# Four layers on one core: linear attention through sums of x by k, q and k by transposition, late mask rows summed

## The chip, the cores and the metric

The kernel runs on one core of a Trainium2 chip. The metric is the device time of the program in microseconds (us), as a median over runs. The core's engines are named here as in the profile: PE (TensorE, matmul) with its weight loads PEld, DVE (VectorE), ACT (ScalarE), POOL (GpSimd) and SP (SyncE, which issues most DMA transfers).

## The reference, cut to what matters

Four layers work in turn on two batches of 1024 tokens with 128 channels. Each computes `x = x + s * silu(ffn(xn))` where `xn` is x after a layernorm without gain and `s` is an attention of xn. Three parts of it matter here.

```python
# layer 1, attention: 16 heads of 8 channels
qkv = (x @ W_qkv + b_qkv).reshape(B, N, 3, H, hd).transpose(2, 0, 3, 1, 4)
q, k, v = (qkv[0], qkv[1], qkv[2])
...
attn = jax.nn.softmax(sim, axis=-1)        # sim: scaled q.k plus a term by head
weighted = jnp.einsum('bhnm,bhmd->bhnd', attn, v)

# layer 2, attention: linear, 16 heads of 64 channels
qf = elu_feature_map(q)
kf = elu_feature_map(k)
kv = jnp.einsum('nshd,nshm->nhmd', kf, v)
z = 1.0 / (jnp.einsum('nlhd,nhd->nlh', qf, jnp.sum(kf, axis=1)) + EPS)
y = jnp.einsum('nlhd,nhmd,nlh->nlhm', qf, kv, z)
out = jnp.einsum('nlhm,hmd->nld', y, Wo) + bo

# layer 2, ffn: 127 chosen tokens attend to each other under a mask
m_sel = m[bidx[:, :, None], sel_idx[:, :, None], sel_idx[:, None, :]]
```

The mask has 512 rows, while the sequence has 1024 tokens: an index above 511 reads row (and column) 511.

## The kernel before

**Recording and issuing.** The program does not issue instructions as its functions run. `Record` notes each operation as a unit (matmuls of one kind in a row make one unit), and `Record.order` (line 569) reads a packed string, `ORDER`, that lists all units in the order in which they are to be issued, with a flag for each evacuation of PSUM that says whether ACT or DVE does it. A second string, `PLACES`, gives every tile its buffer. `Record.issue` (line 585) then issues everything from one line, so the profile shows nearly every instruction under L605, and groups are told apart by the names of tiles. Each engine works through its own queue strictly in that order, and waits by semaphores where another engine's result is needed. So the two strings alone decide how the stages of the two batches lie beside each other: the second batch follows the first, and each layer's attention and ffn are mixed. The same holds for the SP queue, which issues nearly all DMA transfers, and for the POOL queue, which issues the indirect gathers of layer 1's experts.

**Arithmetic.** All products are in fp32, with moving tiles of up to 512 columns. PSUM has eight banks of 128x512 (`C.bank`); `C.half` and `C.arr` are SBUF tiles of 128x1048 and 128x1024 out of 35 buffers, `C.t512` one of 21 tiles of 128x512. `C.mm` is a product `lhsT.T @ rhs`, `C.transpose` a PE transposition against the identity, `C.evac` a copy by ACT or DVE. `cols(t)` is the slice of block t of 128 columns. `xn` holds tokens in partitions, 128 at a time, and `xnT` channels in partitions.

**Layer 1 attention (`l1_attn`, line 1206).** It computes `qt` and `kt`, q and k with tokens in partitions, for norms and maxima that give a scale and a shift for each head. Then `prepare(g)` (line 1302) makes q and k once more, for a group g of four heads, with channels in partitions: head j of the group lies in partitions 32j to 32j+7, row 32j+8 holds a one (k) or the shift (q), the rest zero. It multiplies `xnT` by weights that were padded on the host in this way, two products of 128x512 for q and two for k. `attend(g, q, k)` works through 16 rounds, each of four score products (`sim`, one for a head, 32 rows each), four exponentials on ACT (`e`) and four products with v (`av`). `prepare` of the next group is recorded ahead of `attend` of the present one.

**Layer 2 attention (`l2_attn`, line 1561).** It takes the 1024 head channels in two halves (`hf`), four tiles of two heads each. For each of eight token tiles it makes k (`pk`) and v (`pv`), adds the bias and the feature map to k on DVE and ACT (`kf`), and copies v with a column of ones to SBUF (`vs`). Then follow the q features (`qf`), and for each of the four tiles a sum over the eight token tiles, `pkv`, of k by v and of k alone. DVE adds v's bias, masks it to the diagonal blocks of two heads and makes the weights for the normalizers (`kvn`). `pz` multiplies those by qf; the result `z` goes through DRAM (`zd`), is spread over partitions (`zc`), inverted and read back broadcast (`zb`, two transfers for each tile). Then `nd` multiplies qf by the masked k-v sums, DVE multiplies the product by zb into qf, and `wo` applies the output weights.

**Layer 2 ffn (`l2_ffn`, line 1657).** `sel` has a column for each chosen token and a tile of 128x128 for each of the eight token tiles. The mask's rows are gathered by products `sel.T @ mask` into `mr` (tiles 0 to 3 against the mask's rows, tiles 4 to 7 each against `ml`, a copy of row 511 in all partitions), then transposed, and the columns gathered the same way into `ms`.

**`program` (line 2257)** calls the stages; `stage(l2_attn, weights("l2"), v[1], b, r)` passes `xnT` alone.

Of the kernel before, what the change touches and what calls it, by code (L numbers as in the profile page):

```python
# [21 lines left out]
ALU = mybir.AluOpType  # L22
# [234 lines left out]
def pack_inputs(inputs):  # L257
# [40 lines left out]
    "c-m!I2UrwW*Pb&oTj*7#h$!}oHTH%Yup_a?7NfC8W7McDyE80cODwU)9yRvF*n96W_7)WziYSUmhix<WKljd(@B5yA7ucPdTTXe;Iq$hZVE)R<"  # L298
    "E*-f1OU@qa(Fp(qP)<WEIq9kv+i#Hy74GfnT@`P`bEsZnxN}8hVWD?nKw+q$W<ikM=y3{K-0GZB?Nr93Rg)G&M0;G|W8|SXdZ_5pb!E?^!*iiV"
    "PVw>THJ?|l_oxAU%J!=8X?s)$SU<%HAf8kpPH)JrC@RICK6bBC#aQXV;SsN+(tge}BwFlNt3khN=G_wS+UYCPeDZvzPdYW}Mp$v=>t<O(#XAmY"  # L300
    "c0WHLv|_1IydhTH9CQ2ytp4!_g9zG7U7js`_hX-S@cTgc|F3ZmX68Z={Z_SsNDd^dA3dt?&yK4OgKOX7t8M0*zK6xv&v){IdKZ^Z+509;RQP^+"
    "r(Q6YHZ(kn+gEmYIDESO$AB)iZ;Tln>s9IneAN3g#XwdM^o`2;ZJ290KP)6<ewlSX%+7|TlOo>Rjg{OxXQ>8@$I=NY*#VUyt1`S*BmPUQe~gN)"
    "5q^gM*$N;ud)!)>x(xga`d#|iE3Gk%+JujWZ3FNjC%PAUj7^8|l6Cj{WdnGY0eApUczA8_-dbhdYVUseu=fkgD$tSazY_MZ7+LA@(f#pbeCm%~"
    "G-GXOAwXUgSajsd_JjbXMD;CMEJLAJtI!W)U?{*`xYbb=piuaI%JM1um97;s!VbMio8NW%zK<0?esN*s7D%6ZBK_N=Oyby>+422{$1j_zDG;a2"
    "`m)NW{W%jyuZDf^W+@JDP{GUo1?)@xA;f#kJfF6c7hfw<>_N6)W_-J*&34FbVK=I8HYdK>`{I|6uDE-AqaAgc-bs>jmVUT<JZ{_40Ns(}w*cB-"
    "s@J>A8931Qy2BtgsrP7A>vEHQc-J_7zxMSUY%;7Fzh*BOdT2NHCOrK1EWqJDf%Ru!$lQ4#!Kd)&b7y|t1;>PApLaX+>&Tx*IX5S*E-aWB`o7hT"
    "U_NJ0|A5$*O}o1O_$GEwlS<zE%L43uTmJp*VSK`1*V(%l4i1FA2LOr>e%X6Wysq{P{m=vZ<Dta+?4mQaBEQ0&<EwnJ0zxx*zVO)e4@>-e>-@_i"
    "*Nmr<EE?kDn70UE`~v@XVbT{X(@GryLcn<I#$o9G$t%BE4>={myk8)_Ho)CI+3OxTylO_h{1+FY=;N?=xcB`oeb++}(S7(|ID4pqpaS0#c%SSR"
    "kBmAfs^kQ}r*;0WyBaD#fp32v{hKnR%0d|9wJ5gXB2h_rFg$<Ls6d-zeLi@K-X8)#`WFbk#Y7ba63~CAP2uq+sv-}<<)N*20wnCkU9#b;%^Pl>"
    "$qUTuaTIzU;Q<;|Sv7gC=|FC<!ErCz!>;@M2nTxAE<BwIr~EHBc*xfSo6p_)J|!LDMvJA5?>B8nrJbKhge8hS@h8LcDjyb}P{*%{oA}EjK~*X~"  # L310
    "io5&Ws*iqkp2FmxzgzjwDja;`{(_A!U<xd&wenEny#0BjV2RH+uy}g?4y)m(+uM2aBY57d|9Jh7_DeH+cbh9I`TNJN8-4%ASE^l~nq2C0xZ{O^"
    "AIQ_DZ)+BowZE(I0ukVoe}NMwa(@iigH}^M)m*#de0t3npj7lPvyEOLLb%>W!aHs3aXjuw_meq+l^zGhb}<DJUMVC7^IVs2nF4+aKuM`r(4am2"
    "e<uY7az{m3gV)cy)<iI8m}+_6v+*uiwE1~WBY(X^Dev^<kAf(Q4*V5F)#U<_=cD=3r%?GF^I!xhx=Pu6h~VOLLsfAb4BFT;=t^)MuM;uDww>ud"
    "U^I^5>A<gHBL;fdp`E9<!v=HCm#?dqdboVWJU_yh5gj2UKvWC-%M311RG(5`#pVH`P!e1MF1?4{Q-xBYY)#Hwa7=_num!&HDG@!0PIZbpQ2{5f"
    "*SQoCbgH0+WL0(;_;(?Wys%P%c;L=X0}%;tEb+E^*nWV54Uy1wb1WQnfUyL8oq|YI)gU^<Q6HVc_y2$@3UIYjrmBb{@Gf#bPC48Q-+hku0KUZ2"
    "qbLA{we!4F^vkP2MJ7hYFOTpyx`XqfM^GRr52K+StPiP^`68rFt@D70EDR|1YIZOvucB$!RaXV!eSr9}-JtnAd8Z51kslTj5mmr#|EYu4<VEra"
    "^yPIf1L?EZ=*SDMc(XcB)NBZU8X<T%9iBu)tsm7gs4hX(gGvtdLt%XEF5b(Q9ig-9uU9zcn4r856N(j2568vyLE*oa754oQ_YzjizB>y4S>~9X"
    "yro%#^<!an%D#I#>1oskGBL4=Fk_)E^vuMYexH8?K|QU;secTL9GiarCS2XU;NIwseSe+ZeU!SIRBeE%sU!$~`>^{+!bQS2c`<KNUf)ZTqQChq"
    "e`@bGUf+FJ{~dVfP90Vh(37s`l{!zp*`%(xy1m1-Cmml{Q@+|VW>X}2&ZpM{pIg-)x4AXqwhdZ8Rm{^7DGO&t-yig|XZ2jasB@7~FQZ->?GE42"
    "Gl~0t`r5KY5AVW1Rmk)eJhT0Nj)8E$LVNH^n3Z9SvU#iIqmM_vm+||Qm^#6R1;eEYdsAz6nzy0b?tLS-B*aYV5TX0Jdz{~n!I;2_APxup&)<D}"  # L320
    "M;*R>=+{u#Z{)JEUu_+5072aK$WUe1;DcQc8c2*@fFnW&xTKDN13ksxdL1YW2T<$@oBa_0p7tR-mEaFS`2yl0<U{DF>!a^qzYEbYI>A=iBd#Y2"
    "e+<*%UA3%$B{RINva+kqW|-s(B1IL>#z>a8f?r;hwtb5`UT798Y#s{>6B?wimvo+m7D0^|<&UZ8Z~^%BR8!}8{03i@_>t1%d6QQHAMaf=d-Wue"
    "C)CU?6N!rlFPm4Xhv*b^>Y9lq1f=Zku36a|J=Ll3^UW4K52aqbo%c|5h-yp6Zl#q!2z=0j9}toVV)bMA+sdNyZrs``nIS^Ym0@a7QD)T3$idaB"
    "!osP`2EZ~zmmP!0zYts%aDuKWi}_Q2yiz23{asg3)j*rqr8dADg*<=0)L;{!G{{aAZ`{wN!>A6)3CZ;FBRL_rqU;{E-gK%3lMTf_Vd-`1zodC6"
    "`hKIkO%BykoF1MZ-z?fz5TF$K75fRUOI=Vkmj_WX-6&oT%zhZ9p!nE5K>?en3cjEC_8BjuPJed2T9H1`^JU1ZdXJ*Sx8XKh<8*^Z9x|j7yAN-N"
    "$V@1?a(=@VPrk(aMf1o4I2B7u(`!fH%f8+*G9LrJ{<9Zh22p$+LCE1gLGVt`|LWP|PR6wT^`kfSZup1)-KveZL8Ew=6x}>>;6na!>FYj=Rwp$5"
    "a^K}YmR79kFa+GMg6!qh)@kiB=f8Aqd%E@;e#>gd;TELLw5J!&Rm>JF(}iE*Yz&(1#ikS(e7Qyy*Y;;A$;w1Her#!LnEI}Q;Pb3z@y`}&+4lin"
    "NMs^LR)^<)zKM&zS*cFVJ|H~%9)h+%g_5)1WHh|mDtX<#=wnqMiZ5??O-dgyEU9u<ojNy01UC%bKe`D_?zXSpSU7RIYt;?aLAcfVTxXwmRkyF+"
    ">+{^V`33$$%!tNK`q#Q~cHEfRgU1$p_S>vVO<ut0jiYOQw|wQ~m^)A~0UnP9*t#;zGB>8qj+SR?22HL7p+|ZJ__n%M+Utw14GVUTd0^W4>g1HC"
    ">xD(rhVdH&&-w6RV{!C9p6cSxwPQ~CRcT;<-u2G2QGbM;9P&@~MkBZE#W3#S^Stiz$ZsLVf8eQV6?XNsH@S7D>yg_17xKifChxr4jDJ!m=tzM-"  # L330
    "6m@x@2L)fF|6WwT0@d(){NC1{zl-7Beiy6XAqADPh&bx+RU_bP+vk4yI`eXS&xkeE3S-X3oK+m2d7iz3UAtWR5i8YhRrYvg`wk^JiND$okI4_X"
    "T>ZuME)DPgUBB+0`r9(+`~}_(9(H^8u&6cPeDuWTZ{M_hcEGPcb`<(;@kQ&Z#}@_uF^VgJ+<@3`M#)nS^aZ^$f9#h7y>lx)sJSJ6{}=G0R|-1p"
    "c;ftDA4b{VM%n#sknc3D78XrB41G)dv6#5Z4#rd{s$km<ZEKYj6hl}*zVBo22)@*Dwb!L~m+N|z6@{-I`gT3^_PRc<U>A%5VI3ht-H_^K+adm-"
    "3L{SNr22=3F7f4ieM@4~jo9K>Vk=A!udUC8hn1^ru2;9z*9hNB)>-1*Sw3X}g?^j*M!X9v`?U8G@N=T3O{w**rK0V1-Jx4ECRQujsE*wltGoO`"
    "5K2FdjmTO7%YOSj2Wr^%M4t)n_1omx08Iw2csui_Av^0n4hbG?9)s%Dy;)HYPwj2Q^|j$(t)b6zbe-0W{;|ikcz_&d^bE;&ZeeV@pW3HCoBHff"
    ")5a%4Y=g?Kwktm39CA1V0)w9Uk;$ubY7|Y}+_|D5uVjlF#TO0m<UQozY|*1QqAS4WkgO+LR?J9Fc4h4zv`v?mZ%><j>&<=f;htqaG20f-H7$En"
    "&333YAGq(UuuqP_t+lzpkKqwlTi%40BLA%VquK>!hV<I$k<aRWC<;Gb=fSA5CuK2N#<q{H)qXe`G8)63svG0?fB#Jdp9uiFjCV6yUQdL}b%U;)"
    "_no}&BeI5;_k#}1ynNr+GwMXG+no#USgw9%yO0&T>(IJ47mjQ>B-BW^DK#qQ_$uPf@gdu*eD(c=wef%W^NX&n8K2U@_}sf>^>9Tu=~saDSQK5&"
    "e~N|UUE2-$UKO|WYy9l!ysYJCR|mazv>dd@c*LXWq*<=0-qA2ObwuR}=HSvP%dL}5^H+`a`f2XRI<Ate6*ro|$`OT&BRq1wr%f1LfuG*YFmdUp"
    "tgV@jl}qLr9@Y1pIkfd{36@rWq2wGaOiB5EL4Wm3Pv326UT+Ftg=e0^_Gn0`&W8teL769BK(C@&Nn7X5{=0ewfYK#H>hj;^jA<`?|I<t_>+8`_"  # L340
    "bYYIEdu*{!58gC4`iJwKm$cd*e>00L=gvU9rSTUt=FidbXZ$7~9ef<=@E6xWE#t{&UQV0f<veqhSV#SQ=1kXs(yNaLoqPJN<4)4)uEK~K?Od@|"
    "sd#^Hzt}c$n-(msF|<@U`C#VwE!OILo1HVY?s+odK-<x^PME%4@9E$nxnqYB2g*Eib&+p`qKc&vS&6^C2n@(3$9nkNn!e2UEbe`jc-mqvcI`52"
    "!dmZPPp<Njoqk`jY;ya0>)JIbu9?yB!R$ZxHF5m%9o&L?jwa7*<nkf!1qjytHFDRjg|@x_92poY-21%U-q)Wx$C;gFA2#uSmKhsI?QHP8(fvOo"
    "VdA=4s<F)_P@Cnwel+KmvdZ6V**5d1pBD70bB`BXhI&|VpAMa~qDGJSd8g)ns`=?%*gI&Leydu?8yN!vPPWhSEAfDUyR|OHo#=8u_|f=h_iE>Y"
    "|IOP|CM+&^XsG@quuAi_6>GgHEpxTnIP6BPlI*Y`LlIHmmsJZX@%f``z~wfNE0>1e79Q6Q4*h@$!c|tOGn~q({*DiM;PT@8-&s1z<6e_CD~4}t"
    "z_&f$cz@N{v!cV}Ni{LEYP-v=FEziG{pGHq$2}USw^WO_8i&}0M=kiX&6TGy``TZHdx>YdUUb}U$~&U@C#u5dRU{4g2hfr)dPK;8$MC2|!^~U#"
    "e!n>5h9KBlMRbO56O=dn*OQ{w&HDP==hFcG{8@LpAmh~0Gx;SBp;{aLCLvTOwA}u&#naZ=8ExNYReKY8B{Wj-749}Hd^*f{rtQ`i^}42(W{r4U"
    "6LzY)#vgSpuLimrZ5=-7_p{x~9yWR6uqM|B*XGt1FgLjq{Rnvbhi*@QoYL?gogzWnj7hsc8qyZ#j$bvY3ydo?Iy~*w@9TNLko15F%R+NA=l`jH"
    "QR-D#)BCSz{#9ku;>@MX3O+9T;l~BUzw@yYZ^e5;MceXOKTe(z=(rYEX=&okm}#@-Dxzc*Nzj;qb?3O0O7`JfEi)ZkCU{xD3H()<_$u(1ve+95"
    "ieIVD<EL@{$$iUiDYjVKXAi3DJ##mO@Ks2Wt^e6Pcr*E^&m+FhD|>E(w;{plK3S756<4^aE3J`ba5j1z@UX+h$R0mB3^NBnE86YMntw&+PJ4!L"  # L350
    "h&$2jZqiBqTGACb#dop?<#em`;Uquo&HWzA4zIqUt2*bkTIv<_zUzZ$ap`&bvXJ<VEmWQU9O#X<ru^fg{=(r}p2Eepj>plL1+~SEFO*YdU!4iN"
    "(CM;Ztos<EgMu=J@XX@dIuKg+`$2HDxHoU7ct?#MJikulp5FQA<M=B%p3xOf^!yZjB>vAnxxuRbg|X}TE97|h__|?RQlIBFTds#Xr>k@nvL9qs"
    "YO3&tyA1-iRc<KgZbx7DP&2A{xEf#cwtLi8Z9aFrsy}LUtL^4`21m7uH^s(<&x?$;pXuvGz7&uq|Gnh&GcxJ>CHp>IF%HV>c`d^$CoJyQ+J@Y0"
    "ovZRk5*%oMUZ>DtEOZ*}AOA|I^S1KKHkV&rN#v1t39i#IVR=tOK7->>|KsfzN8>{Bh)M#SccQ&`S9Z{?&&0n9eLCD~CR}oLI9d0-tNBfPE90d$"
# [851 lines left out]
def l1_attn(C, w, xnT, b, out):  # L1206
# [88 lines left out]
    scales, shifts = own[:, :G], own[:, G:]  # L1295

    nc.vector.tensor_scalar(shifts, shifts, C.c["row8"], None, ALU.mult)
    bs = C.small("bs", G)
    nc.vector.tensor_mul(bs, scales, w["bq"])
    nc.vector.tensor_add(shifts, shifts, bs)  # L1300

# [78 lines left out]
def l1_ffn(C, w, xn, xnT, b, out):  # L1380
# [177 lines left out]
    out["g"] = acc  # L1558


def l2_attn(C, w, xnT, b, res):


    nc = C.nc
# [801 lines left out]
```

## Time and profile before

| What | Value |
|---|---|
| Median of 3 runs | 1870.38 us (1868.97 to 1874.28) |
| Profiled execution, its own time | 1864.44 us |
| Its span in the profile | 1862.7 us |
| Mean granted TensorE clock | 0.961 |
| Attention of layer 1, first to last ACT instruction of both batches | 384 to 858 us |
| Attention of layer 2, first product `pv` to last `nd` | 854 to 1118 us |
| Matmul records, DVE, ACT and POOL instructions | 15148, 2819, 1988, 440 |

The profile is of one execution. Its page gives the busy time of each engine, the chain of work that ended last (followed back from the end: at each step to what released it), and the costliest groups of instructions. Further views of the same trace give the busy time of each engine in chosen stretches, the instructions in order of time, and all instructions that touch a named tile. A line of a group has the line of code, engine and operation, then out<-in by tile names with buffer numbers left out, shapes, count, the total busy time and the mean length of one in ns, and the idle time of the engine just before them with what ended it. In the order of time each line has its start, its length, and in square brackets the idle time before it with its releaser. The page says of itself that matmuls are pipelined and their ends modelled, so that a busy PE is not PE at its peak.

### The profile page before, as it was taken

How to read it: one execution, taken by the hardware profiler on the slowest of the kernel's cores; microseconds unless marked ns; L12 is line 12 of the kernel's file. 1: busy time of each engine (PE TensorE's matmuls, PEld its weight loads, DVE VectorE, ACT ScalarE, POOL GpSimd, SP SyncE). 2: the span in 40 equal slices, each digit the busy share in tenths (PEclk: the TensorE clock that was granted, in tenths of full speed). 3: DMA queues.
4: the chain of work that ended last, by engine and by line, in shares of the span. 5: the costliest groups of instructions: out<-in, count | busy, mean ns of one | idle time of the engine just before them, and what ended most of it. 6: DMA issues, size and time to landing. Idle time of an engine off the chain costs nothing.

```text
span 1862.7 us, 37413 instructions
## 1 busy us (share of the span) xinstructions
PE 1739.7 (93%) x15148; PEld 1009.8 (54%) x15148; DVE 1335.7 (72%) x2819; ACT 1070.6 (57%) x1988; POOL 416.3 (22%) x440
## 2 busy tenths in 40 slices
PE   7985899679999999999999999999999999899987
PEld 3464456454225842276666668754446776543566
DVE  6775988686213643246889898889987978978865
ACT  4211443136996588856546556766657757766543
POOL 0001110222222143211301370124214510630000
PEclk9895899588999999999999999999999999999989
DMA  3010011002313321242231222101011110001021
GB/s 126 13 23 4 1 24 25 4 1 66 100 40 114 113 70 41 61 151 75 61 89 48 65 67 64 36 1 48 12 37 44 58 47 25 1 1 40 10 73 35
DMA packets 68301, 88.99 MB, mean 48 GB/s; under 512 B 29568, under 2 KB 41856, under 8 KB 68000
## 3 DMA queue, kind: packets, MB, share of 16 engines
q1 hardware_dynamic: 59008, 57.26, 10.2%
q0 software_dynamic: 9120, 29.33, 5.2%
q8 instruction: 119, 1.95, 0.4%
q14 instruction: 54, 0.44, 0.1%
HBM read 79.62 MB, written 6.95 MB: 46 GB/s over the span
## 4 chain that ended last, share of the span: by engine, by line
PE 79%; DVE 10%; issue 4%; ACT 3%; DMA 1%; POOL 1%; SPq 1%; DVEq 0%; POOLq 0%; ACTq 0%
PE sim L605 16%; PE num L605 8%; PE ph L605 6%; PE av L605 6%; PE wo L605 5%; PE tr L605 4%; PE down L605 3%; PE qk L605 2%; PE up L605 2%; PE z L605 2%; DVE u L605 2%; PE p L605 2%; PE nd L605 1%; PE q L605 1%; PE pu L605 1%
## 5 line engine op out<-in xcount | busy, mean ns | idle before, releaser
L605 ACT ACTIVATE e<-sim 128x512 f32<-128x512 f32 (+3 forms) x896 | 427.7, 559 | 148.1 <-PE sim L605 69.0
L605 PE MATMUL num<-e,v 128*64 128x192 f32 (+4 forms) x1280 | 183.7, 426 | 2.2 <-ACT e L605 2.2
L605 DVE TENSOR_TENSOR e<-e 128x512 f32<-128x512 f32 (+3 forms) x320 | 171.6, 574 | 16.4 <-PE num L605 9.1
L605 PE MATMUL sim<-q,k 32*128 32x512 f32 x1024 | 150.2, 638 | 0.5 <-DVE asb L605 0.5
L605 PE MATMUL sim<-q,kT 64*128 64x512 f32 (+3 forms) x768 | 147.7, 504 | 1.5 <-ACT e L605 1.5
L605 POOL TENSOR_TENSOR sq<-qk,tab 128x256 f32<-128x256 f32 x128 | 98.6, 797 | 219.9 <-DVE ss L605 98.5
L605 PE MATMUL av<-e,va 128*32 128x512 f32 x1024 | 134.9, 603 | 0.0
L605 PEld LDWEIGHTS num<-e,v 128*64 128x64 f32 x1280 | 83.1, 138 | 89.9 <-issue 68.1
L605 ACT ACT_TABLE_LOAD x93 | 119.3, 1283 | 9.0 <-DVE h L605 5.2
L605 PE MATMUL ph<-h,w_f 128*128 128x512 f32 x256 | 119.3, 622 | 0.0
L605 PEld LDWEIGHTS sim<-q,kT 64*128 64x128 f32 x768 | 71.7, 186 | 76.9 <-ACT e L605 36.9
L605 PEld LDWEIGHTS sim<-q,k 32*128 32x128 f32 x1024 | 43.9, 183 | 99.8 <-ACT e L605 74.2
L605 ACT ACTIVATE e<-e 128x320 f32<-128x320 f32 (+3 forms) x160 | 76.9, 530 | 30.3 <-DVE e L605 29.7
L605 POOL TENSOR_TENSOR u<-u,sq 128x512 f32<-128x512 f32 x64 | 89.1, 1411 | 0.9
L605 PEld LDWEIGHTS ph<-h,w_f 128*128 128x128 f32 x256 | 50.2, 200 | 60.9 <-issue 58.6
L605 DVE TENSOR_TENSOR sim<-sim,const 128x128 f32<-128x128 f32 x256 | 64.5, 291 | 25.3 <-PE sim L605 24.4
L605 DVE SCALAR_TENSOR_TENSOR conv<-vT,w_a,conv 128x1024 f32<-128x1024 f32 x60 | 78.3, 1312 | 0.9
L605 POOL DMA_INDIRECT we<-in_experts,index x46 | 44.4, 966 | 135.9 <-DVE index L605 42.7
L605 POOL DMA_INDIRECT xg<-xd,index x46 | 45.0, 977 | 122.7 <-DVE index L605 62.0
L605 DVE TENSOR_REDUCE ss<-sq 128x8 f32<-128x512 f32 x96 | 63.1, 675 | 10.3 <-ACT sq L605 9.9
L605 PEld LDWEIGHTS av<-e,va 128*32 128x32 f32 x1024 | 21.5, 108 | 85.1 <-issue 75.7
L605 DVE SCALAR_TENSOR_TENSOR e<-sim,const 128x320 f32<-128x320 f32 (+2 forms) x128 | 60.6, 528 | 8.7 <-PE sim L605 5.7
(535 smaller groups left out, 3576.2 us busy)
## 6 DMA issues: line engine op xcount, KB each, us to landing
zb<-zd SPq DMA_DIRECT2D x192, 128.0 KB
tab<-in_rotary SPq DMA_DIRECT2D x8, 512.0 KB
yd<-y SPq DMA_DIRECT2D x10, 256.0 KB
w_f<-in_f SPq DMA_DIRECT2D x4, 512.0 KB
mk<-in_mask SPq DMA_DIRECT2D x4, 512.0 KB
w_l<-in_l SPq DMA_DIRECT2D x4, 512.0 KB
w_f<-in_f SPq DMA_DIRECT2D x4, 448.0 KB
const<-in_const SPq DMA_DIRECT2D x1, 1041.5 KB
```

What stands on the lines that cost most here:

```text
L605: tc.keep_in_program_order(f(*map(real, args), **{k: real(v) for k, v in kw.items()}))
```

## The change

It has three parts, and a new order.

**Layer 2 attention.** v is no longer made. Since v is x times its weights, the sum over tokens of k by v is the sum of x by k, put through the weights of v. `pg` sums `xn` by kf over the eight token tiles (one product of 128x512 each), `pn` sums kf alone by products with 32 columns of ones, four of them in different column groups. Both are copied to SBUF (`gT`, `kn`); `pkv` multiplies them by the weights and (a 32nd of) the bias of v; DVE masks all four tiles in one operation (`kvT`); `po` multiplies by the output weights, and the copy `kvo` holds the weights from qf straight to the output. `pc` and `kc` make the weights of the normalizers from `kn`. qf is now multiplied by zb itself, without `nd`, and `wo` multiplies it by `kvo`. The tile `vs`, its ones, and `kvn` go. `l2_attn` also takes `xn`.

**Layer 1 q and k.** `prepare` copies four heads out of `qt` or `kt` into a zeroed tile `wide` (zero fill on GpSimd; for k also a fill of ones at place 8), eight tiles of 128 columns, transposes these on PE, and copies the result: q with scale and shift on DVE as before, k by an evacuation on ACT or DVE. The host still packs the padded weights.

**Masks of late rows.** DVE sums the last four tiles of `sel` into `late`; the four products with `ml`, and the four with `lt`, become one each.

**Order.** `ORDER` and `PLACES` are other strings, for all layers.

```diff
-    bs = C.small("bs", G)
-    nc.vector.tensor_mul(bs, scales, w["bq"])
-    nc.vector.tensor_add(shifts, shifts, bs)
 
     def prepare(g):
 
         q, k = C.arr("q"), C.arr("k")
-        for dst, wn in ((q, "wq"), (k, "wk")):
+        for dst, src in ((q, qt), (k, kt)):
+            wide = C.arr("wide")
+            nc.gpsimd.memset(wide, 0.0)
+            wv = wide.rearrange("p (t j c) -> p t j c", j=J, c=32)
+            if src is kt:
+                nc.gpsimd.memset(wv[:, :, :, 8:9], 1.0)
+            sv = src.rearrange("p (t h d) -> p t h d", h=H, d=8)
+            C.evac(wv[:, :, :, 0:8], sv[:, :, J * g : J * g + J, :])
             for i in range(2):
                 s = cols(i, 1, BLK)
                 ps = C.bank("qk")
-                C.mm(ps, w[wn][:, cols(g)], xnT[:, s])
-                if wn == "wq":
+                for t in range(4):
+                    C.transpose(ps[:, cols(t)], wide[:, cols(4 * i + t)])
+                if src is qt:
                     nc.vector.tensor_scalar(dst[:, s], ps, scales[:, g : g + 1], shifts[:, g : g + 1], ALU.mult, ALU.add)
                 else:
-                    nc.vector.tensor_scalar_add(dst[:, s], ps, w["bk"][:, g : g + 1])
+                    C.evac(dst[:, s], ps)
...
-            pk, pv = C.bank("pk"), C.bank("pv")
-            C.mm(pk, xt, w["wk"][:, hs])
-            C.mm(pv, xt, w["wv"][:, hs])
+            pk = C.bank("pk")
+            C.mm(pk, xnT[:, cols(t)], w["wk"][:, hs])
             k, e = C.t512("k"), C.t512("e")
             nc.vector.tensor_add(k, pk, bk[:, hs])
-            nc.scalar.copy(vs[t // 2][:, t % 2, :, 0:P], pv.rearrange("p (a n) -> p a n", a=4))
             nc.scalar.activation(e, k, AF.Exp, bias=C.c["minus1"])
-            nc.vector.scalar_tensor_tensor(kf[t // 2][:, t % 2, :], e, 1.0, k, ALU.min, ALU.max)
+            nc.vector.scalar_tensor_tensor(kt(t), e, 1.0, k, ALU.min, ALU.max)
+            C.mm(pg, xn[:, cols(t)], kt(t), start=t == 0, stop=t == TB - 1)
+            if t % 4 == 3:
+                for c in range(4):
+                    C.mm(
+                        pn[cols(c, 1, 32)], C.c["ones"][:, :32], kt(t - 3 + c), start=t == 3, stop=t == TB - 1,
+                        tile_position=(0, 32 * c), skip_group_check=True,
+                    )
...
+        gT, kn = C.t512("gT"), C.t512("kn")
+        C.evac(gT, pg)
+        C.evac(kn, pn)
+        pkv = C.bank("pkv")
         for a in range(4):
-            pkv = C.bank("pkv")
-            for t in range(TB):
-                C.mm(
-                    pkv[:, :129], kf[t // 2][:, t % 2, cols(a)], vs[t // 2][:, t % 2, a, :],
-                    start=t == 0, stop=t == TB - 1,
-                )
...
+            C.mm(pkv[:, cols(a)], w["wv"][:, at(a)], gT[:, cols(a)], stop=False)
+            C.mm(pkv[:, cols(a)], bv[:, at(a)], kn[:, cols(a)], start=False)
+        kvT, kvo = C.t512("kvT"), C.t512("kvo")
+        nc.vector.tensor_tensor(tiles(kvT), tiles(pkv), C.c["bo64"].unsqueeze(1).to_broadcast([P, 4, P]), ALU.mult)
+        po = C.bank("po")
+        for a in range(4):
+            C.mm(po[:, cols(a)], kvT[:, cols(a)], w["wo"][:, at(a)])
+        C.evac(kvo, po)
+
+        pc, kc = C.bank("pc"), C.t512("kc")
+        for a in range(4):
+            C.mm(pc[:, cols(a, 1, 32)], kn[:, cols(a)], C.c["mean"][:, :32])
+        nc.vector.scalar_tensor_tensor(
+            kc[:, :P].rearrange("p (a n) -> p a n", a=4), pc[:, :P].rearrange("p (a n) -> p a n", a=4), 4.0,
+            C.c["turns"].unsqueeze(1).to_broadcast([P, 4, 32]), ALU.mult, ALU.mult,
+        )
...
-                C.mm(pz[cols(a, 1, 32)], kvs[a][:, P:], qf[a][:, s], tile_position=(0, 32 * a), skip_group_check=True)
+                C.mm(
+                    pz[cols(a, 1, 32)], kc[:, cols(a, 1, 32)], qf[a][:, s], tile_position=(0, 32 * a), skip_group_check=True
+                )
...
             for a in range(4):
-                C.twice(zbs[i][a], zd[2 * a : 2 * a + 2])
-        for i in range(NB2):
-            s = cols(i, 1, BLK)
-            for a in range(4):
-                ps = C.bank("nd")
-                C.mm(ps, kvs[a][:, :P], qf[a][:, s])
-                nc.vector.tensor_mul(qf[a][:, s], ps, zbs[i][a])
+                za = zb[a // 2][:, cols(a % 2, 1, BLK)]
+                C.twice(za, zd[2 * a : 2 * a + 2])
+                nc.vector.tensor_mul(qf[a][:, s], qf[a][:, s], za)
...
-                    C.mm(
-                        ps[:, cols(k)], qf[a][:, cols(4 * g + k)], w["wo"][:, cols(4 * hf + a)],
-                        start=a == 0, stop=a == 3,
-                    )
+                    C.mm(ps[:, cols(k)], qf[a][:, cols(4 * g + k)], kvo[:, cols(a)], start=a == 0, stop=a == 3)
...
+    late = C.t512("late")[:, :P]
+    nc.vector.tensor_reduce(late, sel[:, 4 * P :].rearrange("p (t n) -> p n t", t=4), X, ALU.add)
     ps = C.bank("mr")
-    for t in range(TB):
-        C.mm(ps, sel[:, cols(t)], mks[t] if t < 4 else ml, start=t == 0, stop=t == TB - 1)
+    for t in range(5):
+        C.mm(ps, sel[:, cols(t)] if t < 4 else late, mks[t] if t < 4 else ml, start=t == 0, stop=t == 4)
...
-    for t in range(TB):
-        C.mm(ps[:, :P], mt[:, cols(t)] if t < 4 else lt, sel[:, cols(t)], start=t == 0, stop=t == TB - 1)
+    for t in range(5):
+        C.mm(ps[:, :P], mt[:, cols(t)] if t < 4 else lt, sel[:, cols(t)] if t < 4 else late, start=t == 0, stop=t == 4)
```

## The prediction

> **What bounds the kernel now.** I read the page's busy shares and its chain that ended last first, then busy time by stage, then the order of time inside two stages, then the groups of the instructions that the change touches.
>
> ```profile
> PE 1739.7 (93%) x15148; PEld 1009.8 (54%) x15148; DVE 1335.7 (72%) x2819; ACT 1070.6 (57%) x1988; POOL 416.3 (22%) x440
> ...
> PE 79%; DVE 10%; issue 4%; ACT 3%; DMA 1%; POOL 1%; SPq 1%; DVEq 0%; POOLq 0%; ACTq 0%
> ```
>
> TensorE holds 79% of the chain. But PE's 93% counts the latency of pipelined records, so stages must be told apart:
>
> ```profile
> 450.00:575.00 125.00, 125.00 (x960) 36.04 (x956) 28.39 (x133) 114.55 (x224) 37.02 (x38) 1.00 0.26 79
> 575.00:650.00 75.00, 75.00 (x605) 58.30 (x602) 40.38 (x100) 42.20 (x70) 9.61 (x12) 1.00 0.36 113
> 650.00:800.00 150.00, 149.48 (x1114) 50.78 (x1112) 57.07 (x147) 125.48 (x239) 52.61 (x53) 1.00 0.20 57
> ...
> 850.00:1125.00 275.00, 268.17 (x1476) 172.93 (x1476) 237.23 (x493) 148.81 (x255) 83.81 (x92) 1.00 0.23 68
> 900.00:1050.00 150.00, 149.66 (x810) 97.62 (x808) 137.44 (x304) 79.86 (x130) 15.64 (x16) 1.00 0.26 76
> ```
>
> Columns: stretch, its us, then PE, PEld, DVE, ACT, POOL busy. In 450 to 575 and 650 to 800 (attention of layer 1) ACT is busy 92% and 84%. In 850 to 1125 (layer 2 and the start of layer 3) DVE is busy 237 of 275 us, and in its densest part, 900 to 1050, 137.4 of 150 us (92%) beside a PE that never pauses: two engines near their limit at once. The order of time in layer 1:
>
> ```profile
> 562.12 0.31 PEld L605 LDWEIGHTS sim<-q,k 32*128 32x128 f32 x8 [0.84 <-ACT e L605]
> 562.13 1.14 PE L605 MATMUL sim<-q,k 32*128 32x512 f32 x8
> ...
> 563.20 1.06 PE L605 MATMUL av<-e,va 128*32 128x512 f32 x8
> ...
> 564.19 0.31 PEld L605 LDWEIGHTS sim<-q,k 32*128 32x128 f32 x8 [0.84 <-ACT e L605]
> ```
>
> A round of scores and sums returns every 2.06 us (562.12 to 564.19), exactly four exponentials at the 0.52 us that ACT needs for one (23 in 11.95 us), and the score waits for ACT. PE's own work in a round, 8 sim and 8 av records four abreast, is 4 x 0.43 = 1.7 us. So in these rounds ACT sets the pace. The durations for the sums:
>
> ```profile
> 924.70 3.44 PE nd L605 x8
> 928.13 3.57 PE pkv L605 x32
> ...
> 906.28 1.92 PE L605 MATMUL pz<-qf,kvn 128*32 128x512 f32 x16 [0.28 <-DVE kvn L605]
> 910.46 0.60 PE L605 MATMUL tr<-const,sel 128*128 128x128 f32 x4
> ```
>
> A product is two records (32 products nd are x64), a transposition one. Spacing in a stream: 3.44/8 = 0.43 us per record of 512 columns, 3.57/32 = 0.112 of 128; four transpositions last 0.60 with a latency of 0.27 each, so (0.60-0.27)/3 = 0.11.
>
> **What the Trainium skill says.** "Perfetto Trace Analysis", section Identifying the Most-Contended Engine: matmul busy time is a bad measure of the limit because matmuls are pipelined. The trace agrees: an nd record lasts 594 ns and follows the last by 430. "TensorE: Matmul & The Clock Gate", section Part 3: Packing small matmuls: outputs of 32 columns in different column groups run together. Agrees: 16 pz records take 1.92 us, four abreast, where 16 nd would take 6.9. "Perfetto Trace Analysis", section Optimizing Scalar/DVE Operations: a DVE operand costs more overhead in PSUM than in SBUF. The trace differs: qf<-nd,zb out of PSUM takes 677 ns, q<-q,zb out of SBUF 744; I use the trace. The same section says that GpSimd and DVE share a port; one kvn operation took 1.02 us in place of 0.24 while GpSimd worked on the mask at 902 to 905.
>
> **Layer 2 attention, PE.** Per half of the columns (four in all: two batches, two halves) out go pv, 8 products x 2 x 0.43 = 6.9 us; pkv, 32 x 2 x 0.112 = 7.1; nd, 8 x 2 x 0.43 = 6.9; together 20.9. In come pg, 6.9; pn, 8 products four abreast, 4 x 0.43 = 1.7; the new pkv, 8 x 2 x 0.112 = 1.8; po 0.9; pc, 0.9 at most (32 columns; lower bound near 0, I take 0.9); together 12.2. Four times 8.7 = **34.8 us less**.
>
> **Masks of late rows, PE.** Per batch three mr products (6 x 0.43) and three ms products (6 x 0.112) go: 3.25, so **6.5 us less** for two.
>
> **Layer 1 q and k, PE.** 32 products of 512 go, 64 x 0.43 = 27.5; 128 transpositions of 0.11 come, 14.1: **13.4 us less**. Were a transposition bound at its 0.275 us latency it would be 35 and a loss of 8, but the trace streams them at 0.11. All PE: 54.7 us.
>
> **What the other engines gain or lose.** Layer 2, DVE: the 48 kvn operations go, 16 x (0.391+0.341+0.287) = 16.3; the 32 multiplications by zb cost 0.067 more each, +2.1; kvT 4 x 0.69, kc 4 x 0.29, bv 2 x 0.68, the late sum 2 x 0.675 (as ss from 512 elements), +6.8; in the built program five evacuations of layer 2's second part stand on ACT and not on DVE, -3.4. Net **-10.8 us**. ACT: 32 copies of v go (0.584 each, 18.7), 12 evacuations of gT, kn, kvo come (7.1), net -11.6, of no worth: ACT is busy 54% there. Layer 1: DVE loses 16 additions to k (11.9) and gains copies, slightly less in all, no matter at 23 to 38% busy. ACT gets 7 of 16 copies of k (0.59) and 9 of 16 into wide (256 elements, not in the trace in this form: 0.37 as qkT from 256, at most 0.59), about **+7 us** on the engine that sets the pace. GpSimd: 16 zero fills of 128x1024 at 0.95 (as td) and 8 of ones at about 0.12, 16 us, less the 16 fills of v. They stand in a queue with gathers that wait for indices (longest wait in 450 to 575: 10.4 us); behind them wait the copies into wide, then q and k of the next group. A group is 16 rounds, 33 us, and the next is prepared ahead of it: covered, at nothing. Without that cover each of 8 groups could lose up to 10 us.
>
> **What reaches the end, layer 2.** PE there shrinks by 41.3, DVE by 10.8, so DVE sets the stretch: (237.2-10.8)/0.92, at the fill that 900 to 1050 shows, is 246 us in place of 275: **29 us**. Bounds: PE's 41 if DVE packs to 0.97, and 13 at the mean fill of today (226/0.863 = 262).
>
> **Layer 1.** All of 13.4 if products of the experts can move from 575 to 650 and 800 to 850, where PE is bound, into the rounds' freed slots; -7 if only ACT's extra work counts. I take **6**, a little above the middle: in the built program more products of the experts stand among the first batch's rounds.
>
> The added waits: the new pkv waits for gT and kn, po for kvT, wo for kvo; what is behind them on PE's queue is the next stage's work. The built order puts other products between the first two; a bare hand-over costs about 1 us (an evacuation of 0.6 and latency), some 4 to 8 us at worst, within the bounds. Layers 0 and 3 do the same work in a new written-out order: 0, with 10 us either way. No DMA is added or taken away. Sum **35 us**: the profiled execution, 1864.4 (span 1862.7), would be 1829. Its time is 5.9 below the median shown, so from 1870.4 the forecast is **1835**.
>
> **Rivals.** (A) As summed: 1835, own range 1823 to 1847. (B) PE bounds everywhere: 1870.4-54.7 = 1816. For it: 79% of the chain. Against: ACT's 2.06 us rounds, DVE's 92%. (C) DVE and ACT take over: layer 2 gives 13, layer 1 nothing: 1857. For it: the same two facts. (D) Slower: the normalizers' way by DMA. From z's copy (908.7) to the first multiplication by zb (930.8) it took 22 us in the first half-layer; the nd products, 6.9 us each half, no longer stand in that gap, and now wo waits directly for the multiplications. With half of it exposed in all four halves, 4 x 11 = 44 us, the time is 1835+44 = 1879; it is slower from about 10 us exposed each (35+5.6 over 4). Against it: in the built order 22 to 40 us of PE work, by the spacings above, lie between the last pz and the first multiplication of every half. (E) It does nothing: the freed PE time turns wholly into waiting for ACT and DVE: 1870.
>
> **How the numbers follow.** About 0.3%, 5.6 us, is what a measurement can tell from no change. Chances: A 0.60, B 0.18, C 0.15, D 0.04, E 0.03. Faster 0.92, same 0.04, slower 0.04. The range takes all of A, B's time with the 7 us below it that a better order could bring, and C: 1809 to 1858.
>
> **What would show it.** Right: MATMUL records go from 15148 to 15060 (layer 2 -128, masks -24, layer 1 +64), and the stretch from the first pk to the last wo of layer 2 shortens by some 30 us with DVE over 90% busy; the rounds of layer 1 keep 2.06 us and the layer shortens by less than 10. Wrong: DVE under 85% there with PE waiting for zb or kvo (D, C), or a PE still without pause in layer 2 (B). Layers 0 or 3 changing by more than 10 us would make the sum wrong whatever layer 2 does.

## The result, and the profile after

| | Before | After |
|---|---|---|
| Median | 1871.51 us (4 runs, 1868.97 to 1874.28) | 1848.69 us (4 runs, 1847.05 to 1849.79) |
| Profiled execution, its span, mean clock | 1864.44, 1862.7, 0.961 | 1849.79, 1848.0, 0.951 |

The ratio of after to before is 0.9877 (95% interval 0.986 to 0.9894): 22.8 us less by the medians, where 35 were forecast. The page of the profile after, busy time and the chain that ended last:

```profile
PE 1705.1 (92%) x15060; PEld 996.9 (54%) x15060; DVE 1319.8 (71%) x2769; ACT 1075.4 (58%) x1999; POOL 444.4 (24%) x448
...
PE 43%; DVE 10%; ACT 2%; DMA 2%; issue 2%; SPq 1%; POOL 0%; DVEq 0%; ACTq 0%; POOLq 0%
```

The 88 records that should go are gone. The chain's shares add up to only some 60%, so its 43% can't be set against the 79% of before. Busy time by stage, columns as in the prediction:

```profile
450.00:575.00 125.00, 123.55 (x922) 42.90 (x920) 37.98 (x137) 112.51 (x221) 37.96 (x38) 0.99 0.25 67
850.00:1125.00 275.00, 261.98 (x1514) 167.55 (x1513) 242.02 (x463) 163.42 (x274) 87.39 (x79) 0.99 0.26 73
900.00:1050.00 150.00, 143.12 (x723) 83.16 (x723) 140.75 (x279) 88.96 (x142) 27.73 (x25) 1.00 0.21 59
```

In 900 to 1050, layer 2, PE, which had no pause before, now pauses for 7 us (and its busy time still counts latency), while DVE is busy for 140.75 of 150 us, 94%. The new operations and layer 1's rounds after, as groups and in order of time:

```profile
L604 PE MATMUL pg<-kf,xn 128*128 128x512 f32 x64 | 33.5, 615 | 4.9 <-DVE kf L604 4.5 <-issue 0.4
L604 DVE TENSOR_TENSOR qf<-qf,zb 128x512 f32<-128x512 f32 x32 | 23.7, 764 | 0.6 <-DMA zb<-zd 0.6
L604 PE MATMUL qk<-const,wide 128*128 128x128 f32 x128 | 19.7, 289 | 0.0
L604 POOL MEMSET wide<- 128x1024 f32 x16 | 15.1, 953 | 43.5 <-PE pu L604 23.9 <-DVE g L604 6.0 <-PE au L604 5.8
```

```profile
529.38 0.31 PEld L604 LDWEIGHTS sim<-q,k 32*128 32x128 f32 x8 [0.84 <-ACT e L604]
...
531.45 0.31 PEld L604 LDWEIGHTS sim<-q,k 32*128 32x128 f32 x8 [0.84 <-ACT e L604]
```

The multiplications by zb waited 0.6 us in all for their transfers, and a round of layer 1 still takes 2.07 us.

**Where the time went.** The table gives the time from one product record's start to the next, put to the layer of the later record; with the norms and the tail the columns add up to the span. "After again" is the changed kernel on a second chip (an experiment below).

| us | Before | After | After again | Forecast of the difference |
|---|---|---|---|---|
| Layer 0 | 374.8 | 394.5 | 389.0 | 0, with 10 either way |
| Layer 1 | 455.8 | 450.6 | 448.1 | -6 |
| Layer 2 | 241.5 | 214.2 | 213.2 | -29 |
| Layer 3 | 762.0 | 758.2 | 761.2 | 0, with 10 either way |
| Span | 1862.7 | 1848.0 | 1841.9 | -35 |

Layers 1 and 2 gave 5.2 and 27.3 us. Layer 0, whose instructions the change doesn't touch, took 19.7 back (14.2 on the second chip). Its order, its buffers and the engine of 30 of its evacuations did change: 19 of them went from ACT to DVE, 11 the other way. The spans differ by 14.7 us and not by the medians' 22.8, since the profiled execution of before was 7 us below its median and that of after 1 above.

**Where in layer 0.** Two places show a loss. For the first, busy time in two stretches, the kernel before and then the changed one; the value behind POOL's is the granted clock:

```profile
200.00:220.00 20.00, 20.00 (x51) 8.15 (x50) 19.56 (x24) 12.78 (x21) 0.99 (x2) 0.99 0.00 0
220.00:240.00 20.00, 20.00 (x89) 12.81 (x89) 18.76 (x21) 7.21 (x9) 1.90 (x1) 0.83 0.01 1
```

```profile
200.00:220.00 20.00, 16.68 (x41) 6.73 (x41) 16.96 (x19) 7.86 (x13) 0.00 (x0) 0.68 0.00 0
220.00:240.00 20.00, 20.00 (x79) 12.70 (x79) 12.52 (x15) 8.14 (x13) 0.00 (x0) 0.81 0.01 1
```

DVE does 38.3 us of work in these 40 us before, and 29.5 after. What DVE waited for from 178 to 245 us, before and after:

```profile
DVE lg L605 <- PE logit L605: 0.3, 1, 0.3
```

```profile
DVE lg L604 <- PE logit L604: 7.0, 1, 7.0
DVE acc L604 <- ACT pad L604: 3.3, 1, 3.3
```

In order of time, before and after:

```profile
219.25 15.81 DVE L605 SCALAR_TENSOR_TENSOR conv<-vT,w_a,conv 128x1024 f32<-128x1024 f32 x12
235.36 0.29 DVE L605 TENSOR_TENSOR lg<-logit,w_a 128x128 f32<-128x128 f32 x1 [0.30 <-PE logit L605]
```

```profile
226.14 1.28 DVE L604 SCALAR_TENSOR_TENSOR conv<-vT,w_a,conv 128x1024 f32<-128x1024 f32 x1
234.39 0.29 DVE L604 TENSOR_TENSOR lg<-logit,w_a 128x128 f32<-128x128 f32 x1 [6.97 <-PE logit L604]
```

In the old order twelve convolution steps of batch 1 fill DVE while PE makes batch 0's logits. In the new one the softmax of the logits (`lg`) stands in DVE's queue ahead of most of them, and DVE idles. PE waits too, for DVE's `fT` (2.3 us) and `feat` (1.0), and loses half of its clock: from 207 to 221 us it ran at 0.50.

```profile
217.71 2.07 PE L604 MATMUL proj<-xnT,w_a 128*128 128x512 f32 x2
```

```profile
211.29 1.02 PE L605 MATMUL rh<-xnT,w_a 128*128 128x512 f32 x2
```

Two records of 512 columns, 2.07 us after and 1.02 before.

This is not the whole loss. The table says when a share of layer 0's PE work was issued, each unit counted at the shortest time that it takes in any of the traces:

| Layer 0's PE work issued | Before, at us | After | After again |
|---|---|---|---|
| 45% | 185.2 | 188.2 | 186.2 |
| 65% | 259.7 | 268.3 | 263.0 |
| 75% | 290.6 | 301.1 | 295.8 |
| 85% | 327.0 | 345.0 | 340.6 |
| all | 436.8 | 455.3 | 449.5 |

The stretch shown above lies between 45% and 65%. It cost 5.6 us in the first trace and only 2.3 in the second, where DVE still waited 5.2 us for the logits. The larger and steadier loss, 7.5 and 8.4 us, lies between 75% and 85%, where batch 1's small products (`pu`, `chunk`) meet the end of batch 0. PE's waits there, before (290.6 to 327 us) and after (301.1 to 345), the two longest of each; "issue" stands for a wait without a releaser in the profile:

```profile
PE pu L605 <- issue: 1.9, 2, 1.5
PE chunk L605 <- issue: 1.1, 1, 1.1
```

```profile
PE chunk L604 <- issue: 4.1, 3, 2.1
PE ph L604 <- ACT h L604: 2.5, 1, 2.5
```

All of PE's waits there add up to 3.7 us before and 8.9 after (9.3 in after again).

### The profile page after: what moved, and what is told of

It is laid out like the page before. It is cut to its first block, busy times and chain, and to the rows that moved or that the text cites. A ratio compares the mean times of both kernels' runs of the same rounds, so it can differ in the third digit from the quotient of the medians.

```text
span 1848.0 us, 37236 instructions
## 1 busy us (share of the span) xinstructions
PE 1705.1 (92%) x15060; PEld 996.9 (54%) x15060; DVE 1319.8 (71%) x2769; ACT 1075.4 (58%) x1999; POOL 444.4 (24%) x448
## 4 chain that ended last, share of the span: by engine, by line
PE 43%; DVE 10%; ACT 2%; DMA 2%; issue 2%; SPq 1%; POOL 0%; DVEq 0%; ACTq 0%; POOLq 0%
PE sim L604 11%; PE num L604 8%; PE wo L604 3%; PE tr L604 2%; PE down L604 2%; PE av L604 2%; DVE u L604 2%; PE z L604 2%; PE q L604 1%; SPq L604 1%; PE qk L604 1%; PE up L604 1%; PE a L604 1%; DVE qf L604 1%; PE g L604 1%
## 5 line engine op out<-in xcount | busy, mean ns | idle before, releaser
L604 PE MATMUL num<-e,v 128*64 128x512 f32 (+4 forms) x1280 | 181.8, 424 | 0.9 <-ACT e L604 0.8
L604 POOL TENSOR_TENSOR sq<-qk,tab 128x256 f32<-128x256 f32 x128 | 106.8, 855 | 224.7 <-DVE ss L604 141.8
L604 PE MATMUL sim<-q,k 32*128 32x512 f32 x1024 | 155.0, 644 | 3.8 <-DVE q L604 3.4
L604 PE MATMUL sim<-q,kT 64*128 64x512 f32 (+3 forms) x768 | 144.0, 504 | 1.8 <-ACT e L604 1.8
L604 PE MATMUL ph<-h,w_f 128*128 128x512 f32 x256 | 114.2, 603 | 3.9 <-ACT h L604 2.5
L604 PEld LDWEIGHTS sim<-q,k 32*128 32x128 f32 x1024 | 49.1, 185 | 95.8 <-ACT e L604 72.4
L604 PE MATMUL qk<-w_f,shifted 128*128 128x512 f32 x128 | 64.6, 630 | 4.6 <-ACT sq L604 4.4
```

Of the source, the lines that this page charges most:

```text
L604: tc.keep_in_program_order(f(*map(real, args), **{k: real(v) for k, v in kw.items()}))
```

## The experiments

Both kernels record the same first 1108 units, the whole of layer 0 and the start of layer 1; only `ORDER` and `PLACES` treat them differently. So each order can be tried in the other kernel. The edits to the order are made in these packed strings, and their diffs are told in words. The strings hold the order, the choice between ACT and DVE and the buffers together: no experiment takes these apart, and "order" below means all three.

**1. Layer 0 in the old order, in the changed kernel.**

```diff
-ORDER: all units as in the changed kernel
+ORDER: layer 0's units as in the kernel before, all later ones merged in by their times in the changed kernel
```

> The changed kernel with all units of layer 0 (and the norms and weight loads up to it) in the order, on the engines and in the buffers that they had before; the units of layers 1 to 3 keep the changed kernel's sequence. No arithmetic differs. Theory 1 (the new written-out order of layer 0 gives back 18 to 20 us of the gain; in the trace, PE time that falls to layer 0 went from 375 to 395 us): 1830 us, 1825 to 1836, with the last product of layer 0 back at about 436 us. Rival (layer 0 differs by chance between the two profiled executions, or what it loses is made up again at the border to layer 1): 1849 us, within 5.

Measured: 1850.7 us, 0.9916 of before (0.989 to 0.9941). Layer 0 fell to 383.0, layer 1 rose to 460.8: a miss for the theory as to the whole. At the border to layer 1 the merged order waits for layer 1's scales and shifts, with the tail of layer 0 queued behind that wait; PE's waits from 380 to 450 us:

```profile
PE tr L592 <- DVE par L592: 12.0, 1, 12.0
```

**2. The reverse: the new order of layer 0 in the kernel before.**

```diff
-ORDER: all units as in the kernel before
+ORDER: layer 0's units as in the changed kernel, all later ones merged in by their times in the kernel before
```

> The kernel before with the units of layer 0 in the changed kernel's order, engines and buffers; layers 1 to 3 as before. Theory 1: slower by 18 to 20 us, 1890 us (1884 to 1895). Rival (layer 0's order is not the cause): 1871 us, within 5.

Measured: 1934.68 us, 1.0371 (1.0342 to 1.0401). Layer 0 took 410.4 and layer 1 490.8. Neither figure fits. That the merge itself did the damage is likely, as layer 1 lost 35 us beside layer 0's 36, but no run shows it alone.

**3. The sums of x by k twice.**

```diff
-            C.mm(pg, xn[:, cols(t)], kt(t), start=t == 0, stop=t == TB - 1)
+            C.mm(pg, xn[:, cols(t)], kt(t), start=t == 0, stop=False)
+            C.mm(pg, xn[:, cols(t)], kt(t), start=False, stop=t == TB - 1)
```

> The changed kernel with every product of the sum of x by k (pg) made twice into the same bank, so that this sum comes out doubled: 32 more products, 64 records of 0.43 us = 27.5 us more of PE work in layer 2's attention, nothing more on DVE or ACT, the order unchanged. Theory 1 (DVE sets the pace of layer 2 after the change: busy 97.0 of 100 us between 925 and 1025): most of it disappears in PE's pauses, +5 to +14 us, about 1858 us. Rival (PE sets the pace there too): +24 to +28 us, 1875 us.

Measured: 1861.83 us, 0.9988 (0.9972 to 1.0003), 21 us above the changed kernel's ratio; layer 2 rose by 21.4 us against after again. Between the two figures, nearer to the rival's. DVE's waits over layer 2 in this kernel, and in the changed one:

```profile
DVE k L604 <- PE pk L604: 25.0, 20, 3.6
```

```profile
DVE k L604 <- PE pk L604: 3.6, 4, 1.5
```

Of PE's added 27.5 us all but some 6 reached the end: so little had PE in hand.

**4. Copies of layer 1's q and k on DVE.** 16 flags in `ORDER`.

```diff
-16 evacuations of wide and k in layer 1: ACT
+16 evacuations of wide and k in layer 1: DVE
```

> The changed kernel with the 16 copies of layer 1's q and k that stand on ACT (9 into wide at 0.39 us, 7 of k at 0.59 us, 7.6 us together) given to DVE, which is busy under a half there; the order unchanged. Theory 1 (ACT sets the pace of layer 1's rounds): 4 to 8 us faster, about 1843 us. Rival (PE or the gathers set the pace of layer 1): no change, 1849 within 2.

Measured: 1861.24 us, 0.9978 (0.9962 to 0.9994). Both theories missed: layer 1 took 466.0 us, some 15 more. Two places in its trace, first a wait of the scores that ended at 443 us, then three of DVE's instructions in order of time:

```profile
PEld sim L593 <- DVE q L593: 6.0, 1, 6.0
```

```profile
505.36 0.15 DVE L593 COPY index<-token 128x1 int32<-128x1 int32 x1 [6.46 <-DMA xg<-xd,index]
505.43 0.28 DVE L593 COPY wide<-qt 128x256 f32<-128x256 f32 x1
...
514.90 0.69 DVE L593 COPY k<-qk 128x512 f32<-128x512 f32 x1 [9.12 <-PE qk L593]
```

The first came where DVE was full: from 425 to 443 us it was busy for 17.6 of 18 us, with the end of layer 0. In the second DVE had time, but a copy into `wide` stood in its queue behind an index for the experts' gathers, which waited for a transfer, and then DVE waited 9.1 us for the products of the next copy. The mean busy share of the receiving engine had said nothing of either. How the 15 us divide between the two is not shown.

**5. The changed kernel again, on a second chip.** No edit.

> The changed kernel again, as the measure beside which the other three of this group stand on their chip. Every theory: 18 to 26 us under the kernel before, and in its trace layer 0 takes some 20 us of PE time more than before, as in the first profile. If layer 0 comes out within 5 us of before here, the loss in layer 0 was chance.

Measured: 1842.16 us, 0.9877 (0.9853 to 0.9901), the same ratio; its layers stand in the table above.

**6. Layer 2's parts alone.** The old layer 1 attention, and before's order for layers 0 and 1.

```diff
-layer 1 attention and the order of layers 0 and 1: as changed
+layer 1 attention and the order of layers 0 and 1: as before
```

> Layer 2's part of the change and the masks alone: layers 0 and 1 with the kernel before's code, order, engines and buffers (q and k of layer 1 through the padded weights), layers 2 and 3 with the changed kernel's code and sequence. Theory 1 (layer 2's part brings what its stage shows, 27 us, and what was lost was lost in the new order of layers 0 and 1): 27 to 31 us under the kernel before, so 5 to 10 us under the changed kernel. Rival (the gain of layer 2 needs what the new order of layer 1 prepares for it): 12 to 18 us under the kernel before, slower than the changed kernel.

Measured: 1868.23 us, 1.0018 (1.0003 to 1.0033): no gain, so a miss for both, though on the rival's side. Layer 0 took 375.0 us, as before; layer 2 gained only 12.1, and layer 1 lost 20.5, most of it behind 730 us, where layer 2 runs beside it and the two orders were merged. That layer 2's gain needs an order made for it fits, and so does damage by the merge; the run doesn't tell them apart.

**7. The old order up to the start of layer 1's rounds.**

```diff
-ORDER: all units as in the changed kernel
+ORDER: the first 1108 units as in the kernel before, all later ones merged in by their times in the changed kernel
```

> As the first hybrid, but the old order goes on through the start of layer 1 for the first batch (norm, q and k with tokens in partitions, the chain to scale and shift), which in the first hybrid left PE waiting 12.4 us for that chain with layer 0's tail queued behind it. Theory 1 (the new order of layer 0 and its border to layer 1 costs the loss): 10 to 18 us under the changed kernel. Rival (the end of layer 1's rounds is set by their own order and gathers, whenever layer 0 ends: in the first hybrid layer 0 was 27 us ahead at 320 us and level with the changed kernel at 670): within 5 us of the changed kernel.

Measured: 1844.66 us, 0.9899 (0.9868 to 0.993), within 3 us of the changed kernel beside it, as the rival said. In its trace layer 0 took 398.0 us, but batch 0's part of it ended at 302.1 us, as in the kernel before; what was won by then was lost by the end of the layer. The trace is of a run of 1854.88 us, 10 above the median, so its 398.0 may be too long.

**8. k without its bias, to unload DVE.**

```diff
-            nc.vector.tensor_add(k, pk, bk[:, hs])
-            nc.scalar.activation(e, k, AF.Exp, bias=C.c["minus1"])
-            nc.vector.scalar_tensor_tensor(kt(t), e, 1.0, k, ALU.min, ALU.max)
+            nc.scalar.activation(k, pk, AF.Relu, scale=-1.0)
+            nc.scalar.activation(e, k, AF.Exp, scale=-1.0)
+            nc.vector.scalar_tensor_tensor(kt(t), pk, 1.0, e, ALU.add, ALU.max)
```

> The changed kernel, in layer 2's attention without the bias of k: the 32 additions of it on DVE (0.68 us, 21.8 us) go, and the feature map of k is made as that of q is, with 32 more activations on ACT (0.69 us, 22 us), which is busy under two thirds there. PE work and order as before. Theory 1 (DVE sets the pace of layer 2 after the change): 12 to 20 us faster than the changed kernel. Rival (PE and DVE bind together, since the doubled products passed on some 12 of their 27.5 us): 3 to 8 us faster. Rival (PE alone): no change.

Measured: 1889.57 us, 1.0123 (1.007 to 1.0175), 47 us more than the changed kernel beside it. Inconclusive on DVE's rate. The way from `pk` to `kf` still has three operations, but the first two now stand in ACT's queue, and `pk`'s bank is held until the last. DVE then waited for ACT, over layer 2 in this kernel and in the changed one:

```profile
DVE kf L593 <- ACT e L593: 33.3, 18, 8.5
```

```profile
DVE kf L604 <- ACT e L604: 3.3, 3, 1.5
```

DVE was busy in only 105.6 of 150 us from 900 to 1050.

**9. The old order joined to the new one where both have done the same.**

```diff
-ORDER: all units as in the changed kernel
+ORDER: the units that the kernel before has issued by its 380 us, in that order, then the rest in the changed kernel's own order
```

> The changed kernel, all of its work kept, with the one thing altered that its first 380 us of layer 0 follow the written-out order of the kernel before (same instructions, same engines, same buffers there). The two orders have done almost the same set of instructions when the kernel before is at 380 us and the changed one at 398 us (the sets differ by 4.3 us of work), so the one can be cut and the other joined without a mix of the two. Theory 1 (the new order of layer 0 costs the 15 to 20 us that are missing): 15 to 18 us less than the changed kernel, about 0.978 to 0.980 of the kernel before where the changed one has 0.9877, and the last product of batch 0's first layer back at about 300 us from 321 to 325. Rival (the time of layer 0 is lent by work that is done early there, and is paid back later in any order): the changed kernel's time, 0.987 to 0.989. Anything slower says that the joint itself disturbs.

Measured: 1845.04 us, 0.9905 (0.988 to 0.9929): a miss for the theory's time. Its trace has both sides. Layer 0 took 373.9 us, the old figure; batch 0's part ended at 299.1 us, and DVE no longer idled for the logits:

```profile
DVE lg L593 <- PE logit L593: 0.3, 1, 0.3
```

But layer 1 took 459.6 us, 11.5 more than in after again, 7.1 of it in one wait just behind the joint (PE's waits, 370 to 440 us):

```profile
PE wq L593 <- DVE qt L593: 7.1, 1, 7.1
```

The traced run took 1834.31 us at a mean clock of 0.957; the other four 1842.71 to 1850.23 at 0.946 to 0.950, and where those lost their clock no trace shows.

**10. Half of the multiplications by the normalizers.**

```diff
-                nc.vector.tensor_mul(qf[a][:, s], qf[a][:, s], za)
+                h = cols(2 * i, 1, BLK // 2)
+                nc.vector.tensor_mul(qf[a][:, h], qf[a][:, h], za[:, : BLK // 2])
```

> The changed kernel with the 32 multiplications of layer 2 by the normalizers done on 256 of their 512 columns (half of q is left without its normalizer); the number and order of the instructions stay. About 32 x 0.35 = 11 us less work on DVE in layer 2, PE's work unchanged. Theory 1 (DVE sets layer 2's pace): 8 to 11 us less than the changed kernel, 0.982 to 0.984 of the kernel before. Rival (PE sets it again since the change): within 2 us of the changed kernel, 0.987 to 0.988.

Measured: 0.9849 of before (0.9823 to 0.9874), 5 us below the changed kernel's ratio with intervals that overlap. The edit took 8.2 us from DVE (23.7 to 15.5), not 11. The traced run had a lower clock in layer 0 (405.4 us there), so only its layer 2 is read: 212.7 us against 213.2, less than the 1.0 us between the two traces of the changed kernel. The medians don't decide, but the layer's own time speaks against theory 1.

**11. Most of the sums of x by k over half the columns.**

```diff
-            C.mm(pg, xn[:, cols(t)], kt(t), start=t == 0, stop=t == TB - 1)
+            n = BLK if t == 0 else BLK // 2
+            C.mm(pg[:, :n], xn[:, cols(t)], kt(t)[:, :n], start=t == 0, stop=t == TB - 1)
```

> The changed kernel with 28 of the 32 products that sum x by k in layer 2 taken over 256 of their 512 columns (the other half of the sums keeps only its first block); the number and order of the instructions stay. 28 x 2 records x 0.215 us = 12 us less work on PE in layer 2, DVE's work unchanged. Theory 1 (DVE sets layer 2's pace): within 3 us of the changed kernel, 0.986 to 0.988 of the kernel before. Rival (PE sets it again since the change): 9 to 12 us less, 0.981 to 0.983.

Measured: 1841.58 us, 0.9869 (0.9843 to 0.9896), as theory 1 said; layer 2 took 211.9 us, 1.3 less, for 12 us less of PE work. PE's waits over layer 2 in this kernel, and in the changed one:

```profile
PE pg L604 <- DVE kf L604: 7.1, 9, 1.3
PE pz L604 <- DVE kc L604: 3.3, 1, 3.3
```

```profile
PE pg L604 <- DVE kf L604: 4.0, 6, 1.2
PE pz L604 <- DVE kc L604: 2.5, 1, 2.5
```

So nearly 11 of the freed 12 us turned into waits for DVE, as in these lines, and into wider gaps between PE's records.

**12. The reverse joint.**

```diff
-ORDER: all units as in the kernel before
+ORDER: the units of layers 0 and 1 that the changed kernel has issued by its 390 us, in that order, then the rest in the old order
```

> The reverse of the last joint: the kernel before, all of its work kept, with the one thing altered that its first layer follows the written-out order of the changed kernel up to that one's 390 us, and goes on in its own order from where that stood at 370 us (the sets done by then differ by 7.9 us of work). Theory (the new order is slower for layer 0 whatever follows): layer 0 takes 14 to 20 us more in the trace than the 375 us of the kernel before, and the whole 12 to 20 us more, 1.006 to 1.011 of it. Rival (the new order lends time to layer 1, and the sum is neutral): layer 0 longer by as much, but layer 1 shorter by about the same, and the whole within 4 us of the kernel before, 0.998 to 1.002. As the other joint waited some 7 us for a late operation, up to 7 us above the theory's figure would be the joint's.

Measured: 1898.94 us, 1.0173 (1.0126 to 1.022), 30 us more than the kernel before beside it. Layer 0 took 408.8 us, 34 more; 8.3 of them are a wait at the joint (PE's waits, 345 to 500 us):

```profile
PE rh L594 <- DVE xnT L594: 8.3, 1, 8.3
```

Ahead of the joint, batch 0's part of layer 0 ended at 328.6 us, 27.8 later than before. Layer 1 gave nothing back (457.4 against 455.8). The rival, time only lent, fell; the theory's sign held and its size was too small.

**Layer 0 over all runs.** In the five traces with the old order at the start (before, experiments 1, 6, 7, 9) batch 0's part of layer 0 ends at 298.3 to 302.8 us. In the nine with the new one (after, 2 to 5, 8, 10 to 12) it ends at 320.1 to 328.6. This end tells which order a kernel follows, as the new one puts batch 0's last products behind some of batch 1's; the loss is told by the whole layer's time.

## Why the prediction was right, and where it was not

- **The number.** 1848.7 us lies in the stated range of 1809 to 1858, but 2 us above the range of the sum itself (A, to 1847). The stated range reached so far for C, in which layer 2 gives 13 us and layer 1 nothing. Neither happened: what filled that room was a loss in layer 0, which the sum had put at nothing. That the time still fell inside is luck. By the prediction's own sign (layer 0 or 3 moving by more than 10 us) the sum was wrong.
- **Arithmetic of PE's work: right.** Records fell from 15148 to 15060. By the spacings, layer 2 needs 41.0 us less (41.3 forecast) and layer 1 13.4 less. In DVE's list kvT, kc, bv and the late sum make 6.6 and not 6.8, which changes nothing.
- **Layer 2, DVE sets the pace, 29 us: right in size, the reason not shown.** 27.3 us, with DVE 94% busy in the densest part. Experiment 11 shows that less PE work no longer helps there, which rules out rival B; experiment 3 shows that most of what is added reaches the end. But less work on DVE brought the layer 0.5 us for 8.2 (10). Neither engine alone sets the pace, then: a near tie, or the waits that the written order puts between them; the runs don't say which. From the first `pk` to the last `wo` it was 276.5 before and 255.2 after: 21 and not 30, because layers 1 and 3 have other work in that stretch.
- **Layer 1, ACT sets the pace, 6 us: right in size, the reason not shown.** 5.2 us, and 7.7 on the second chip; the rounds kept their 2.07 us in both kernels. Taking ACT's copies away (4) made the layer longer, so no run confirms the reason. The cover for GpSimd's fills held (16 of 0.953 us, 16 us forecast): no copy into `wide` waited for them.
- **The normalizers' way (rival D): did not happen.** 0.6 us of waiting for zb in place of the 44 that it needed.
- **The shared port.** The prediction set one kvn operation of 1.02 us beside GpSimd's work on the mask. It fell into that work (GpSimd from 904.87 to 907.92 us), but another, at 903.67 us, took its usual 0.24 while GpSimd worked from 902.28 to 904.64. No term rested on it.
- **The step that failed: "Layers 0 and 3 do the same work in a new written-out order: 0, with 10 us either way."** Layer 3 kept to it (3.8 less, 0.8 on the second chip). Layer 0 lost 19.7 us (14.2), up to twice the bound. Without this loss the spans would differ by 34.4 us (35.0). The same units need 374 to 375 us in the old order (before, experiments 6 and 9; 383 and 398 where a merge lay at the layer's end) and 389 or more in the new one, and experiments 9 and 12 show that in both kernels it goes with the order. A part could have been looked for ahead: in the old profile DVE is 96% busy from 200 to 240 us, where an order that lets its queue wait can lose time. But that stretch holds only 2 to 6 us of the loss; the larger part lies behind it: in the old profile at 290 to 327 us, where DVE was busy for 27.3 of 37 us only. I had treated unchanged instructions as unchanged time.

That layer 0's order costs layer 0 this much is shown. That the whole would be so much faster with the old one is not: in experiment 9's trace 11.5 of the 15 us were lost again in layer 1, and the median did not gain. Whether an order exists that keeps both is open; of all kernels that do the whole work, the changed one has the lowest ratio to the kernel before. How much of layer 0's loss is waiting and how much PE's half clock is not separated either, as the one lengthens the other; nor is the order from the choice of engines.

## What to carry to other kernels

Where the issue order is written out by hand, a new order is a change to every layer. Compare the two orders stage by stage in the traces, by the time at which equal work was issued. Stages in which one engine is over 90% busy are a first place to look, as an instruction that waits at the head of such a queue holds ready work behind it; here they held the smaller part of the loss. And an order is tuned as one piece: part of one put before part of another paid at the joint in three of the runs here (7 to 12 us in one wait), so such hybrids tell where time sits better than what the whole would gain.

## What the runs showed of the hardware

TensorE's clock has two values in these traces, 1.00 and 0.50, and changes in steps of 3.4 us. "TensorE: Matmul & The Clock Gate", section Part 1: The HAM clock gate of the Trainium skill, describes this gate: half rate unless a window of about 3.4 us was busy. The traces agree in the values and the step, and give the price for fp32: a record of 512 columns comes every 0.429 us at full clock and every 0.853 at half, one of 128 columns 0.111 and 0.213. Layer 0's smallest records, of 32 rows and 32 columns (`au`, `chunk`), lengthen less, by about 15 to 25%: for `au` 10.6 ns a record at full clock, 13.3 at half. In the first 470 us the kernel before spent 126 us at half clock, after 154, after again 143.

Not expected was how much this can move one and the same program. Experiment 7's five runs took 1843.17 to 1844.66 us at a mean clock of 0.952 to 0.953, or 1854.65 to 1854.88 at 0.945 to 0.946. A clock lower by 0.007 over 1850 us is 13 us of clock time, about the 11 us between the two groups. That the one causes the other was not tried.
